# One gated add for each expert in the token mixer of a two-layer convolution and attention kernel

## The chip, the core and the metric

The kernel runs on one core of a Trainium2 chip. Its time is the device time of one execution, in microseconds (us). The numbers of the profile come from one profiled execution, and its own time stands beside them below.

## What is computed

The reference takes four images of 64 x 64 pixels with 128 channels and sends them through two layers. The first is a gated residual convolution block with a causal attention over the 4096 pixels. The second is an attention with 16 heads, a gated feed-forward part, and a mixture of 8 experts. The change is in the last of these:

```python
router_probs = jax.nn.softmax(x @ router_w + router_b, axis=-1)
top_p, top_i = jax.lax.top_k(router_probs, K)          # K = 2 of E = 8
top_p = top_p / jnp.sum(top_p, axis=-1, keepdims=True)
expert_out = jnp.einsum('bnd,edc->bnec', x, expert_w) + expert_b
gathered = jnp.take_along_axis(expert_out, top_i[..., None], axis=2)
return jnp.einsum('bnk,bnkc->bnc', top_p, gathered)
```

The kernel does not gather. It multiplies each token with all 8 experts' matrices, weights the 8 products with a row of 8 gates of which six are zero, and adds them to the token.

## The kernel before

**Work and tiles.** `fast_path` (L116) does one image at a time. An image is cut into 8 chunks of 512 tokens, so there are 32 chunks in all. Attention scores are computed for 128 keys and 512 queries and four heads at once: one step (`attention_step`, L832) has four score matmuls into two tiles `s` of 1024 columns, two exponentials on ScalarE (`e<-s`), and four value matmuls into `acc`.

**PSUM.** There are three tiles `s` of two banks each (`s_tile`, L138), one bank `acc`, and **one** bank `m` (`m_tile`, L141). All other matrix products (projections, the feed-forward part, the experts) go through this one bank while attention runs: `bank()` (L162) gives `m`, except when nothing runs beside, where it gives half of a tile `s`.

**Order.** The order of every engine is written out: the class `InOrder` (L95) makes each operation follow the one issued before it on its engine. Every operation is recorded there, so all rows of the profile carry line 105, and the reader goes by the names of the tiles. The main loop (L1224 to L1263) emits attention steps. For each it issues the scores (`do_step`, L230), then perhaps one piece of other work (`insert`, L247), and then the value products of the step two before (`finish`, L234). Which steps get a piece is decided by a budget of assumed costs when the program is built. It doesn't depend on what VectorE does with the piece.

**A chunk's last part.** `last_part` (L913) is a generator that gives such pieces. For the experts (L1021 to L1037) it takes each of the chunk's four blocks `k` of 128 tokens, and of each two halves of four experts. `halves` (L294) multiplies the 128 tokens with 512 columns of weights as two pieces of 256 columns, in two successive attention steps, and `product` (L280) cuts each into four matmuls of 32 output rows. After the second piece the bank `m` holds a 128 x 512 product, and VectorE reads it. The bank can be written again when VectorE has read it: the next piece belongs to the next half, or to the products with `eb` that end the chunk. Thirty-one of the 32 chunks run beside attention; the last of the last image runs alone at the end.

**VectorE on a product.** The 128 x 512 product is multiplied with the gates, broadcast along the channels, and written to `by_e` in SBUF. After the second half a sum over the 8 experts (a strided reduction of 128 x 1024 to 128 x 128) writes `added`, and an addition puts `added` on the tokens `t`. `by_e` shares its buffer with the tile `two` of `second_operands` (L662), and `added` with the tiles of tag `w`.

Of the kernel before, what the change touches and what calls it, by code (L numbers as in the profile page):

```python
# [9 lines left out]
FP = mybir.dt.float32  # L10
FR = mybir.dt.float32r
AF = mybir.ActivationFunctionType
ALU = mybir.AluOpType
AX = mybir.AxisListType

P = 128
C = 128
# [18 lines left out]
NE = 8  # L36
# [79 lines left out]
def fast_path(ctx: ExitStack, tc: tile.TileContext, a: dict, where: dict, out: bass.AP, verdict):  # L116
# [9 lines left out]
    pe, dve, act, pool, sp = (InOrder(tc, e) for e in (nc.tensor, nc.vector, nc.scalar, nc.gpsimd, nc.sync))  # L126
# [4 lines left out]
    wk = ctx.enter_context(tc.tile_pool(name="f_wk", bufs=2))  # L131
# [9 lines left out]
    def m_tile():  # L141
        return ps_m.tile([P, QB], FP, tag="m", name="m")
# [7 lines left out]
    def chunk(tag, name=None):  # L150
        return wk.tile([P, QB], FP, tag=tag, bufs=CHUNKS.get(tag, 1), name=name or tag)
# [4 lines left out]
    def by_k(ap):  # L156
        return ap.rearrange("p (k c) -> p k c", k=4)
# [4 lines left out]
    def bank():  # L162
        return s_tile()[:, :QB] if alone[0] else m_tile()
# [130 lines left out]
    def halves(ps, lhs, rhs, size=P):  # L294

        for h in range(2):
            cols = slice(h * QB // 2, (h + 1) * QB // 2)
            product(ps[:size, cols], lhs, rhs[:, cols])
            if h == 0:
                yield 0.46, "held"  # L300
# [531 lines left out]
    def attention_step(b, seg, kt, place, qx, vg, part):  # L832
# [19 lines left out]
        def values(es):  # L852
            for j in range(NSLOT):
                pe.matmul(
                    acc[j * SLOT : j * SLOT + 1 + HD1, :],
                    lhsT=vg[:, kt // 4, kt % 4, j, :],
                    rhs=es[j // 2][:, (j % 2) * QB : (j % 2 + 1) * QB],
                    start=kt == seg.lo,
                    stop=kt == seg.hi - 1,
                )  # L860
            if kt == seg.hi - 1:
                at = chunk("at1")
                if part:
                    dve.tensor_tensor(at, acc, part[0], ALU.add)
                else:
                    dve.tensor_copy(at, acc)
                to = scratch[b]["a"][c, g] if seg.hi == NT else scratch[b]["p"][g, c]
                sp.dma_start(out=to, in_=at)
                if seg.hi == NT and g == NG1 - 1:
                    fillers.append([last_part(b, c), LAST, (b, c), False])  # L870
# [36 lines left out]
    def fetch_following(b, c):  # L907
        keys = [part[2] for part in fillers]
        at = keys.index((b, c)) + 1
        if at < len(keys) and keys[at]:  # L910
            fetch(*keys[at])

    def last_part(b, c):  # L913
# [4 lines left out]
        ps = bank()  # L918
# [5 lines left out]
        ps = bank()  # L924
# [6 lines left out]
        for n, (lo, size) in enumerate(FCH):  # L931
            ps = bank()
# [5 lines left out]
            ps = bank()  # L938
# [4 lines left out]
        ps = bank()  # L943
        for m in range(4 * len(FCH)):
            k, n = divmod(m, len(FCH))
# [17 lines left out]
        ps = bank()  # L963
# [4 lines left out]
        ps = bank()  # L968
# [42 lines left out]
        gate = gates[:, :, :NE]  # L1011
# [8 lines left out]
            sp.dma_start(out=g8.rearrange("e (k b a) -> b e k a", k=4, a=SLOT)[b_], in_=by_block[b_, :NE])  # L1020
        for k in range(4):  # L1021
            tk = t[:, k * C : (k + 1) * C]
            by_e = wk.tile([P, NE, C], FP, tag="two", bufs=1, name="by_e")
            for half in range(2):
                ps = bank()
                yield from halves(ps, yT[:, k * P : (k + 1) * P], we_f[:, half * QB : (half + 1) * QB])
                dve.tensor_tensor(
                    by_e[:, 4 * half : 4 * half + 4, :],
                    by_k(ps),
                    gate[:, k, 4 * half : 4 * half + 4].unsqueeze(2).to_broadcast([P, 4, C]),  # L1030
                    ALU.mult,
                )
                if half == 1:
                    added = chunk("w", "added")[:, :C]
                    dve.tensor_reduce(added, by_e.rearrange("p e c -> p c e"), AX.X, ALU.add)
                    dve.tensor_tensor(tk, tk, added, ALU.add)
                fetch_following(b, c)  # L1037
                yield 0.46, "stop"
        ps = bank()
# [279 lines left out]
    ps = m_tile()  # L1319
# [5 lines left out]
    ps = m_tile()  # L1325
# [703 lines left out]
```

## Time and profile before

| | |
|---|---|
| median of three executions | 8155.83 us (8154.7 to 8157.08) |
| the profiled execution's own time | 8154.99 us |
| its span, first to last instruction | 8153.2 us |
| granted TensorE clock | 0.993 |
| busy: PE (TensorE matmul) | 7997.1 us, 98% |
| busy: ACT (ScalarE) | 7866.4 us, 96% |
| busy: DVE (VectorE) | 2415.5 us, 30% |
| busy: POOL (GpSimd) | 646.2 us, 8% |
| products `by_e<-m` beside attention | 248 of 692 ns |
| products `by_e<-s` at the end | 8 |
| sums `added<-by_e` | 128 of 1994 ns |
| additions `t<-t,added` | 128 of 293 ns |

A row of the profile names the engine, the operation, the tile written and the tiles read, the shapes (partitions x elements), how many there are, the busy time in us and the mean of one in ns. Behind the second bar stands how long the engine was idle just before these instructions, and which instruction ended most of that. PE's matmuls overlap, so a busy PE says little by itself; start times say more. In a timeline a row has its start and its length in us, and equal instructions that follow each other are merged (x8). PEld is the load of weights that goes ahead of a matmul. SPq issues the DMAs.

### The profile page before, as it was taken

The numbers are of one execution on the slowest core, as the hardware profiler recorded it, in microseconds if no ns is written. First come the engines' busy times: TensorE is split into PE (matmuls) and PEld (weight loads), VectorE is DVE, ScalarE is ACT, GpSimd is POOL, SyncE is SP. The second block draws the span as 40 slices with busy tenths as digits, with TensorE's granted clock in tenths as the row PEclk, the third lists the DMA queues.
The fourth block names the chain that finished last, engine by engine and source line by source line (L and its number), as shares of the span: only waits on it lengthen the run. The fifth ranks groups of instructions, "written<-read, shape, count | busy, mean of one in ns | idle before, by whom it ended". The sixth has DMA issues, their size and how long they took to land.

```text
span 8153.2 us, 172350 instructions
## 1 busy us (share of the span) xinstructions
PE 7997.1 (98%) x73041; PEld 2477.0 (30%) x73041; DVE 2415.5 (30%) x5001; ACT 7866.4 (96%) x8683; POOL 646.2 (8%) x592
## 2 busy tenths in 40 slices
PE   7999999999999999999999999999999999999998
PEld 3232222223333322233333332222333333232333
DVE  4333222322322232333332223333333332121123
ACT  1899999999999999999999999999999999999996
POOL 1211101000000021110000002111000000000000
PEclk9999999999999999999999999999999999999998
DMA  2221010111100000011110100101111111111121
GB/s 72 68 66 66 25 45 27 53 34 47 49 24 25 30 22 29 33 42 42 43 41 18 38 18 25 36 22 48 36 47 50 49 43 50 37 41 38 61 66 34
DMA packets 213936, 334.18 MB, mean 41 GB/s; under 512 B 31555, under 2 KB 107811, under 8 KB 213155
## 3 DMA queue, kind: packets, MB, share of 16 engines
q1 hardware_dynamic: 209139, 321.31, 12.1%
q8 instruction: 574, 9.40, 0.5%
q10 hardware_dynamic: 4016, 1.77, 0.1%
q14 instruction: 207, 1.70, 0.1%
HBM read 195.09 MB, written 127.93 MB: 40 GB/s over the span
## 4 chain that ended last, share of the span: by engine, by line
PE 90%; issue 6%; ACT 2%; DVE 1%; DMA 1%; POOL 1%; SPq 0%; ACTq 0%; POOLq 0%; DVEq 0%
PE acc L105 43%; PE s L105 29%; PE m L105 18%; ACT e L105 1%; DVE h L105 0%; DMA f_kx<-d_k 0%; POOL rs L105 0%; DVE at L105 0%; POOL xt L105 0%; ACT t L105 0%; DMA xe<-in_x_dram 0%; SPq L105 0%; ACT neg L105 0%; DVE added L105 0%; DMA taps<-in_L_conv_W_dram 0%
## 5 line engine op out<-in xcount | busy, mean ns | idle before, releaser
L105 ACT ACTIVATE e<-s 128x1024 f32<-128x1024 f32 x8480 | 7807.1, 1110 | 81.7 <-PE s L105 75.9
L105 PE MATMUL acc<-e,vg 128*9 128x512 f32 x32768 | 4334.6, 595 | 1.4 <-DVE at L105 1.4
L105 PE MATMUL s<-qx,f_kx 32*128 32x512 f32 (+1 forms) x16960 | 2890.3, 495 | 48.5 <-ACT e L105 25.9
L105 PEld LDWEIGHTS s<-qx,f_kx 32*128 32x128 f32 (+1 forms) x16960 | 1163.5, 181 | 4080.7 <-ACT e L105 3858.7
L105 PEld LDWEIGHTS acc<-e,vg 128*9 128x9 f32 x32768 | 718.4, 90 | 793.9 <-issue 456.0
L105 PE MATMUL m<-v,f_wino 128*32 128x256 f32 x5376 | 429.9, 391 | 7.3 <-POOL v L105 7.3
L105 DVE TENSOR_TENSOR by_e<-m,gates 128x512 f32<-128x512 f32 x248 | 171.5, 692 | 741.0 <-PE m L105 737.8
L105 PE MATMUL m<-f_we,y2T 128*32 128x256 f32 x3968 | 316.9, 391 | 0.5 <-DVE by_e L105 0.5
L105 POOL TENSOR_TENSOR v<-r 128x1024 f32<-128x1024 f32 x112 | 216.7, 1941 | 1264.4 <-PE m L105 1264.0
L105 DVE COPY sd<-m 128x512 f32<-128x512 f32 x168 | 116.2, 692 | 670.7 <-PE m L105 670.7
L105 POOL TENSOR_TENSOR rs<-ve,f_minus_half 128x4 f32<-128x4 f32 x64 | 65.3, 1020 | 3148.0 <-DVE ve L105 3148.0
L105 DVE COPY at<-acc 128x512 f32<-128x512 f32 x131 | 90.6, 692 | 691.5 <-PE acc L105 691.5
L105 DVE TENSOR_REDUCE added<-by_e 128x128 f32<-128x1024 f32 x128 | 255.2, 1994 | 4.8 <-DMA d_g<-turned 0.5
L105 PE MATMUL m<-hT,f_fw 128*32 128x256 f32 (+1 forms) x2728 | 236.0, 391 | 0.0
L105 POOL TENSOR_TENSOR t<-t,h 128x512 f32<-128x512 f32 x32 | 41.0, 1281 | 2036.8 <-DVE h L105 2036.8
L105 DVE TENSOR_TENSOR t<-m,sums 128x256 f32<-128x256 f32 x126 | 53.5, 425 | 493.5 <-PE m L105 493.5
L105 DVE SCALAR_TENSOR_TENSOR h<-m,h 128x512 f32<-128x512 f32 (+1 forms) x93 | 64.2, 690 | 426.9 <-ACT th L105 265.8
L105 DVE COPY h<-m 128x512 f32<-128x512 f32 (+1 forms) x93 | 64.2, 690 | 371.3 <-PE m L105 371.3
L105 DVE TENSOR_TENSOR t<-m,t 128x512 f32<-128x512 f32 x62 | 42.9, 692 | 436.7 <-PE m L105 436.7
L105 PEld LDWEIGHTS m<-v,f_wino 128*32 128x32 f32 x5376 | 105.8, 108 | 172.2 <-issue 144.3
L105 PE MATMUL m<-e,f_v 128*32 128x512 f32 (+1 forms) x1104 | 146.5, 574 | 0.0
L105 DVE TENSOR_TENSOR e<-e,f_consts 128x128 f32<-128x128 f32 x128 | 29.1, 287 | 338.8 <-ACT e L105 338.8
(250 smaller groups left out, 3308.3 us busy)
## 6 DMA issues: line engine op xcount, KB each, us to landing
f_kx<-d_k SPq DMA_DIRECT2D x139, 512.0 KB
qx<-d_q SPq DMA_DIRECT2D x152, 256.0 KB
d_q<-two SPq DMA_DIRECT2D x64, 512.0 KB
d_a<-at SPq DMA_DIRECT2D x128, 256.0 KB
vg<-d_v SPq DMA_DIRECT2D x32, 576.0 KB
d_k<-two SPq DMA_DIRECT2D x32, 512.0 KB
d_v<-vc SPq DMA_DIRECT2D x32, 288.0 KB
xe<-in_x_dram SPq DMA_DIRECT2D x32, 256.0 KB
```

What stands on the lines that cost most here:

```text
L105: made = op(*args, **kw)
```

## The change

The product and the sum are replaced: each expert's 128 x 128 part of the bank is multiplied with the token's gate for it and added to the tokens `t` in place, in one `scalar_tensor_tensor`. There are four of these for each half. `by_e` and `added` are gone. TensorE, ScalarE, GpSimd and the DMA queues have the same instructions in the same order as before. In the built program each of the last three operations of a half waits on a VectorE semaphore for the one before it, because it reads the `t` that this one wrote, and the next matmul into the bank waits for the fourth.

```diff
         for k in range(4):
             tk = t[:, k * C : (k + 1) * C]
-            by_e = wk.tile([P, NE, C], FP, tag="two", bufs=1, name="by_e")
             for half in range(2):
                 ps = bank()
                 yield from halves(ps, yT[:, k * P : (k + 1) * P], we_f[:, half * QB : (half + 1) * QB])
-                dve.tensor_tensor(
-                    by_e[:, 4 * half : 4 * half + 4, :],
-                    by_k(ps),
-                    gate[:, k, 4 * half : 4 * half + 4].unsqueeze(2).to_broadcast([P, 4, C]),
-                    ALU.mult,
-                )
-                if half == 1:
-                    added = chunk("w", "added")[:, :C]
-                    dve.tensor_reduce(added, by_e.rearrange("p e c -> p c e"), AX.X, ALU.add)
-                    dve.tensor_tensor(tk, tk, added, ALU.add)
+                for e in range(4):
+                    at = 4 * half + e
+                    dve.scalar_tensor_tensor(
+                        tk, ps[:, e * C : (e + 1) * C], gate[:, k, at : at + 1], tk, ALU.mult, ALU.add
+                    )
                 fetch_following(b, c)
                 yield 0.46, "stop"
```

## The prediction, on record before the changed kernel ran

> **What bounds the kernel now.** I read the page's busy times first, then its chain, then the timeline around the products that change.
>
> ```profile
> PE 7997.1 (98%) x73041; PEld 2477.0 (30%) x73041; DVE 2415.5 (30%) x5001; ACT 7866.4 (96%) x8683; POOL 646.2 (8%) x592
> ...
> PE 90%; issue 6%; ACT 2%; DVE 1%; DMA 1%; POOL 1%; SPq 0%; ACTq 0%; POOLq 0%; DVEq 0%
> ...
> L105 DVE TENSOR_TENSOR by_e<-m,gates 128x512 f32<-128x512 f32 x248 | 171.5, 692 | 741.0 <-PE m L105 737.8
> ...
> L105 DVE TENSOR_REDUCE added<-by_e 128x128 f32<-128x1024 f32 x128 | 255.2, 1994 | 4.8 <-DMA d_g<-turned 0.5
> ```
>
> PE and ACT share the bound: attention hands scores from one to the other. DVE is busy for 30% and on 1% of the chain, so less work on DVE is worth nothing by itself. What counts is when DVE lets go of something that PE waits for, and here that is the single bank `m`. The timeline of an ordinary expert product:
>
> ```profile
> 2142.68 0.51 PE L105 MATMUL s<-qx,f_kx 32*128 32x512 f32 x4
> ...
> 2143.12 0.64 PE L105 MATMUL m<-f_we,y2T 128*32 128x256 f32 x8
> ...
> 2143.58 1.04 PE L105 MATMUL acc<-e,vg 128*9 128x512 f32 x8
> 2143.83 0.69 DVE L105 TENSOR_TENSOR by_e<-m,gates 128x512 f32<-128x512 f32 x1 [3.04 <-PE m L105]
> ...
> 2144.55 0.51 PE L105 MATMUL s<-qx,f_kx 32*128 32x512 f32 x4
> ...
> 2144.98 0.64 PE L105 MATMUL m<-f_we,y2T 128*32 128x256 f32 x8
> ```
>
> PE's starts run 2142.68 scores, 2143.12 the piece into `m`, 2143.58 values, 2144.55 scores again: no hole, 1.87 us a step. ACT's two exponentials need less: their starts are 0.904 us apart when ACT has its input (the 25th percentile over all of them is 0.904), so 1.81 us. In steps that carry a piece PE is the bound. And the bank: DVE starts to read at 2143.83, PE writes it again at 2144.98, **1.15 us later**. Reading takes 0.69, so 0.46 us are to spare.
>
> **The change, part by part.**
>
> *What goes.* Per block of 128 tokens, two products, a sum and an addition: 2 x 0.692 + 1.994 + 0.293 = 3.67 us of DVE. *What comes.* Eight gated adds. The trace has the same operation on the same shapes, where a token is corrected from the bank (`xt<-m,rs,xt`):
>
> ```profile
> L105 DVE SCALAR_TENSOR_TENSOR xt<-m,rs,xt 128x128 f32<-128x128 f32 x116 | 35.4, 347 | 2.0
> ```
> ```profile
> 218.73 0.17 DVE L105 RECIPROCAL rs<-rs 128x2 f32<-128x2 f32 x1
> 218.94 0.61 DVE L105 SCALAR_TENSOR_TENSOR xt<-m,rs,xt 128x128 f32<-128x128 f32 x2
> ```
>
> The second row holds two that don't depend on each other: 0.61 us for both, so they overlap (0.351 and 0.343 long, the second started 0.267 after the first). The new ones are a chain through `t`, each with a wait. The nearest row of a waiting one is the first of each such pair, which waits for the reciprocal: it starts 0.035 us after that ends and takes 0.351 (58 cases). A sum and its addition show the same 0.035. So a half takes 4 x 0.351 + 3 x 0.035 = **1.509 us instead of 0.692**. Over all 128 blocks DVE is busy 8 x 0.351 = 2.81 instead of 3.67 us each, 110 us less; cover: it idles 70%, so this is worth nothing.
>
> The bank is therefore held longer, although DVE does less. After DVE's last read PE's next matmul starts 0.054 us later, wherever it really waited (26 reads of `m`, 0.053 to 0.055). From the start of reading to the earliest next write: 1.509 + 0.054 = 1.563 us. Where the next write came after 1.155 us, it is now late by **0.408 us**.
>
> *How many.* From the trace's start times I took, for each of the 248 products, the time to the next matmul into `m`: 118 have 1.0 to 1.16 us, one has 0.71, 104 have 2.8 to 3.1 and 25 more than 4.6 (there the schedule leaves a step without a piece). The last 129 have room for 1.56 us and cost nothing.
>
> *Who waits behind.* PE works in order: behind the late piece stand the values of an earlier step and the scores of the next, for which ACT waits. Whether that delay reaches the end is answered by the one product that was read late:
>
> ```profile
> 7911.85 0.50 PE L105 MATMUL s<-qx,f_kx 32*128 32x512 f32 x4
> ...
> 7912.18 0.65 DVE L105 TENSOR_TENSOR by_e<-m,gates 128x512 f32<-128x512 f32 x1
> ...
> 7912.88 0.64 PE L105 MATMUL m<-f_we,y2T 128*32 128x256 f32 x8 [0.53 <-DVE by_e L105]
> ...
> 7914.31 0.51 PE L105 MATMUL s<-qx,f_kx 32*128 32x512 f32 x4
> ...
> 7914.91 1.02 ACT L105 ACTIVATE e<-s 128x1024 f32<-128x1024 f32 x1 [0.41 <-PE s L105]
> ```
>
> PE's piece was due at 7911.85 + 0.44 = 7912.29 and came at 7912.88, 0.59 late. The next scores came 2.46 instead of 1.87 us after the last, 0.59 late, and ACT's exponentials started 1.536 instead of 0.941 us apart, 0.595 late. Nothing was absorbed. Is ACT as starved elsewhere? In 111 of the 119 places the next exponential starts within 0.61 us of the start of its score matmuls, as soon as they are done; in eight it starts 0.01 to 0.28 us later than that, which absorbs 0.9 us together. ACT, once idle, can't make it up: outside these steps it is the bound itself.
>
> So: 118 x 0.408 + (1.563 - 0.708) - 0.9 = 48.1 us more.
>
> *The end.* The last chunk runs alone, and there DVE is the chain: its first product starts at 8130.91 and the last addition ends at 8145.20, 14.29 us. The new chain of 32 adds takes 32 x 0.351 + 31 x 0.035 = 12.32: **2.0 us less**, if PE keeps up, which it does with two pieces of about 0.5 us for each half of 1.54.
>
> *What else moves.* No DMA, no matmul and no exponential changes its place. The buffers of `by_e` and `added` are free; only 0.5 us of DVE idle time was ever put down to them (the DMA of `d_g`), at the end, and it is in the 2.0. The next `m` matmul now has two waits, one in PE's sequencer ahead of it. PE's sequencer passes 540 such waits in this trace, the load behind starts 0.013 us after one (median); I take 0 and keep 0 to 0.16 us for it (0.16 is the whole weight load `m<-f_we` of the timeline). For the pitch of the chain I take 0.386 us; 0.267, the pair without a wait, is the lower end.
>
> *Sum.* 48.1 - 2.0 = +46.1 us on the profiled execution's 8154.99 (its span is 8153.2; it lies 0.8 below the median of the three runs, 8155.83): **8201 us**, 0.56% slower.
>
> *Against the skill.* The trace has 0.267 us between adds without a wait and 0.386 with one. The Trainium skill (VectorE: DVE Perf Modes, "The DRAIN you can't avoid") reports eight copies taking the same time with a semaphore after each and after the last alone, so that the wait "costs nothing extra here". By that rule a half would take 3 x 0.267 + 0.343 and the sum would be the first rival's. The row is of this very operation, so I go by it. The same page's section "The TRN2 errata" gives 120 cycles plus one for each element for a read of PSUM at 0.96 GHz; an estimate from it is 0.258 us for 128 elements, where the rows show 0.347 to 0.351. Four would be 1.03 us, inside the 1.15, and the kernel would gain about 6 us at the end.
>
> **The rivals.**
>
> 1. *The adds overlap* (not slower). If they went at 0.267 us, a half would end at 3 x 0.267 + 0.343 + 0.054 = 1.198 us, late by 0.043: 118 x 0.043 + 0.49 = 5.6 us, less what ACT absorbs, about 0.3; the end would gain 14.29 - (31 x 0.267 + 0.343) = 5.7. Net -0.4: 8154.6 us. It decides at a pitch of 0.253 us, where no product is late. For it: the pair of 0.61 us. Against: the built program has a wait at each.
> 2. *Half of the delay is absorbed*, because ACT after a late step meets a PE that gets ahead again in the next step without a piece. 24 - 2 = +22: 8177 us. Against: ACT's starved starts, and 7914.91.
> 3. *The stall costs PE more than the wait*, with the weight load no longer hidden or the double wait dear: up to 119 x 0.16 = 19 us more: 8220 us. For it: PE had its loads ahead in ordinary steps. Against: in the step of 7912.88 the values follow after 0.46 us, as always.
> 4. *DVE's relief counts* (faster): what PE's loads for `m` waited on `added` (12.7 us, 52 times) and on `at` (28.9 us, 95 times), both late behind sums of 1.99 us, goes, with the 2.0 of the end and no new wait: 8154.99 - 43.6 = 8111 us. Against: these waits are 0.24 and 0.30 us apiece, in front of a PE that is still busy with the step before.
>
> **How the numbers follow.** Forecast 0.68; rivals 0.08, 0.10, 0.12 and 0.02. Forecast and rivals 2 and 3 are slower by over 0.2% (16 us, about what a measurement of this kernel can tell from no change): 0.90. Same 0.08, faster 0.02. The range goes from just below rival 2 to rival 3, 8175 to 8220, and leaves out rivals 1 and 4 and the outer parts of 2 and 3.
>
> **What would show it.** A row of 992 gated adds `t<-m,gates,t` at 351 ns. In tight steps, adds 0.386 apart and the next `m` matmul 1.56 us after the first of them, with scores 2.27 instead of 1.87 us apart. PE's `m` waiting on DVE `t` about 119 times for 0.4 us. ACT idle on PE `s` some 25 us more than now: of the 0.595 us at 7914.91 the profile shows 0.41 as idle, so 0.408 will show as about 0.2. No change where 2.9 us lie between. I am wrong if the adds start before the one in front has ended, or if ACT's exponentials keep their 0.941 us in tight steps.

## The result, and the profile after

The changed kernel takes **8206.58 us** (median of four executions, 8205.69 to 8209.05), the kernel before beside it 8156.45 (four, 8154.7 to 8161.35). The ratio is 1.0062, with a 95% interval of 1.005 to 1.0074: 50 us, or 0.6%, slower. The forecast was 8201 us, 46 us slower.

The profiled execution after has 8205.69 us and a span of 8203.9 us, 50.7 more than before, at the same granted clock of 0.993. Its page, the busy times, the shares of the chain and the group of the new operation:

```profile
PE 8000.4 (98%) x73041; PEld 2485.2 (30%) x73041; DVE 2305.7 (28%) x5513; ACT 7877.1 (96%) x8683; POOL 646.1 (8%) x592
...
PE 88%; issue 6%; DVE 3%; ACT 2%; DMA 1%; POOL 1%; SPq 0%; ACTq 0%; DVEq 0%; POOLq 0%
...
L105 DVE SCALAR_TENSOR_TENSOR t<-m,gates,t 128x128 f32<-128x128 f32 x992 | 348.1, 351 | 847.1 <-PE m L105 817.4
```

DVE is busy for 110 us less than before, as forecast, and the kernel is 50 us slower. The busy times can't show that; only DVE's share of the chain does, which rose from 1 to 3%. The timeline of one half whose bank is written again in the next step:

```profile
2140.31 1.51 DVE L105 SCALAR_TENSOR_TENSOR t<-m,gates,t 128x128 f32<-128x128 f32 x4
...
2141.03 0.51 PE L105 MATMUL s<-qx,f_kx 32*128 32x512 f32 x4
...
2141.96 0.64 PE L105 MATMUL m<-f_we,y2T 128*32 128x256 f32 x8 [0.43 <-DVE t L105]
...
2142.39 1.07 PE L105 MATMUL acc<-e,vg 128*9 128x512 f32 x8
...
2143.39 0.51 PE L105 MATMUL s<-qx,f_kx 32*128 32x512 f32 x4
```

Four adds hold the bank for 1.51 us from 2140.31 on. PE, which wrote `m` again 1.15 us after the first read before, now does so after 1.65 us (2141.96), and everything behind it in PE's order is late: scores are 2.36 us apart (2141.03, 2143.39) instead of 1.87. From the waits of after, in us in total, times and the longest:

```profile
PE m L105 <- DVE t L105: 46.2, 105, 1.4
```

PE waits 0.44 us for the adds on average in 105 places, and hands the delay on to ACT, whose idle time on `s` rose from 75.9 us in 24 places to 120.7 in 140. The 14 other short places, where products with `eb` follow, are listed as waits of `m` on `s`: 5.4 us in 14 places, of which there are none before.

**Where the 50.7 us are.** I set the 8480 exponentials `e<-s`, which come in the same order in both traces, against each other, and took the growth of the difference between their starts.

| stretch | after minus before, us |
|---|---|
| 119 tight places (next write of `m` under 1.2 us after the read began) | +56.7 (median 0.498 each) |
| 129 loose places | +0.03 |
| the rest of the stream | -3.4 |
| before the first exponential | +0.2 |
| from the start of the last exponential on | -2.8 |

I don't put the -3.4 us down to the change. At 4944 and at 5318 to 5323 us the profiled execution of before has short stretches that are about 2.0 us longer than in the profile of `long_one` below and 4.1 us longer than in that of `long_halves`, neither of which changes anything there. In the profile of after they are about 2.5 us shorter than in that of before, which is most of the -3.4. One is a DMA wait (ACT for `xe`, 1.69 us); the cause at 5320 stays open.

### The profile page after: what moved, and what is told of

It reads as the page before. It is cut to its first block, busy times and chain, and to the rows that moved or that the text cites. A ratio compares the mean times of both kernels' runs of the same rounds, so it can differ in the third digit from the quotient of the medians.

```text
span 8203.9 us, 173097 instructions
## 1 busy us (share of the span) xinstructions
PE 8000.4 (98%) x73041; PEld 2485.2 (30%) x73041; DVE 2305.7 (28%) x5513; ACT 7877.1 (96%) x8683; POOL 646.1 (8%) x592
## 4 chain that ended last, share of the span: by engine, by line
PE 88%; issue 6%; DVE 3%; ACT 2%; DMA 1%; POOL 1%; SPq 0%; ACTq 0%; DVEq 0%; POOLq 0%
PE acc L105 41%; PE s L105 29%; PE m L105 18%; DVE t L105 2%; ACT e L105 1%; DVE h L105 0%; DMA f_kx<-d_k 0%; POOL rs L105 0%; DVE at L105 0%; POOL xt L105 0%; ACT t L105 0%; ACT neg L105 0%; SPq L105 0%; DMA xe<-in_x_dram 0%; DMA taps<-in_L_conv_W_dram 0%
## 5 line engine op out<-in xcount | busy, mean ns | idle before, releaser
L105 ACT ACTIVATE e<-s 128x1024 f32<-128x1024 f32 x8480 | 7817.9, 1108 | 125.9 <-PE s L105 120.7
L105 DVE SCALAR_TENSOR_TENSOR t<-m,gates,t 128x128 f32<-128x128 f32 x992 | 348.1, 351 | 847.1 <-PE m L105 817.4
L105 PEld LDWEIGHTS m<-f_we,y2T 128*32 128x32 f32 x3968 | 81.1, 107 | 172.1 <-issue 88.5
```

The source lines that it names most:

```text
L105: made = op(*args, **kw)
```

## The experiments

The theory: time is lost because the single bank `m` is held past the next write, and the number of VectorE operations, their waits and their sum cost nothing in themselves. The rival: the chain of waiting adds, or the wait in PE's sequencer, costs something of its own. Each diff is shortened and against the changed kernel unless it says otherwise; all kernels compute the whole result.

**1. `copy_first`: the same four adds, but out of SBUF.**

```diff
+held = wk.tile([P, 2, QB], FP, tag="two", bufs=1, name="held")[:, half, :]
+dve.tensor_copy(held, ps)
 for e in range(4):                      # reads held[...] instead of ps[...]
```

> The bank m is copied to SBUF in one operation of 128x512 (0.692 us), and the four gated adds then read the copy. VectorE has more to do than in either kernel and as many dependent adds as the changed one. If the time is lost because the bank is held (bank theory), the next matmul finds it free after 0.69 us as before the change: no late step, only the end grows, by 8 x (0.69 + 4 x 0.35 + 4 x 0.035) - 14.3 = 3.6 us: about 8160 us. If it is lost to the number of VectorE's operations or their waits, wherever the bank stands (rival): 8206 us or more.

Measured: 8160.99 us, ratio 1.0006 (0.9996 to 1.0015). The timeline of the same half:

```profile
2141.56 0.69 DVE L105 COPY held<-m 128x512 f32<-128x512 f32 x1
...
2142.28 1.51 DVE L105 SCALAR_TENSOR_TENSOR t<-held,gates,t 128x128 f32<-128x128 f32 x4
...
2142.71 0.64 PE L105 MATMUL m<-f_we,y2T 128*32 128x256 f32 x8
```

The chain of four is still there and still takes 1.51 us. But PE writes the bank 1.15 us after the copy began, while the adds run. The tight places cost 0.1 us in total and the whole stream 0.3; of the 5.0 us that the span is longer, 4.0 lie behind the last exponential, in the last chunk, where DVE is the chain and has the copies to do as well, and 0.7 ahead of the first, where the edit changes nothing. The loss is the bank's, not the chain's. The Trainium skill (VectorE: DVE Perf Modes, "Rules for kernel authors") advises to copy a product to SBUF first when many operations read it. The run agrees with the advice, though not by faster reads: an add takes 352 ns from SBUF and 351 from the bank. What the copy buys is the early release.

**2. `read_twice`: the kernel before, with its product computed twice.** The second writes the same values over the first. No gated add is in it.

```diff
+for _ in range(2):
     dve.tensor_tensor(by_e[...], by_k(ps), gate[...], ALU.mult)
```

> The kernel before, with each product by_e taken from the bank twice, the second overwriting the first; the values stay the same. There are no gated adds. Bank theory: held for 0.692 + 0.035 + 0.692 = 1.419 us; where PE's next matmul has two waits (105 tight places) it is late by 1.419 + 0.145 - 1.155 = 0.41 us, in the 14 with one by 0.32: 47 us, and some 6 us at the end, where VectorE is the chain: 8209 us. Rival, that the chain of dependent adds or 512 more operations cost the time: these are only 256 more, 8156 to 8162 us, or half the loss, about 8180.

Measured: 8203.41 us, ratio 1.0059 (1.0044 to 1.0075), and 45.4 us in the tight places (47 expected; the whole is 5.6 us under the expectation). Two reads hold the bank for 1.42 us, and the loss is back without the change. The theory and this number need no chain of adds at all.

**3 and 4. `two_chains` and `two_chains_own`: two independent chains.** The odd experts go to a tile `odd`, added to the tokens once per block, so that an add waits for the one before the last. The third kernel takes the buffer for `odd` from the tag `w`, the fourth that of the old `by_e`.

```diff
+if half == 0:
+    odd = chunk("w", "odd")[:, :C]                   # two_chains
+    odd = wk.tile([P, 2, QB], FP, tag="two", bufs=1, name="odd")[:, 0, :C]   # two_chains_own
 for e in range(4):
...
+    if e % 2 == 0:
         dve.scalar_tensor_tensor(tk, part, g, tk, ALU.mult, ALU.add)
+    elif at == 1:
+        dve.tensor_scalar(odd, part, g, None, ALU.mult)
+    else:
+        dve.scalar_tensor_tensor(odd, part, g, odd, ALU.mult, ALU.add)
+if half == 1:
+    dve.tensor_tensor(tk, tk, odd, ALU.add)
```

> The changed kernel, but the adds of odd experts go to a second tile that is added to the tokens once for each block: each add depends on the one two before it. Bank theory with the pitch of the unwaited pair (0.267 us): held for 3 x 0.267 + 0.343 = 1.144 us, late by 0.13 us in 105 places and 0.04 in 14, 15 us, and 4 us less at the end: 8167 us. If a wait costs its 0.035 us and the overlap even where its producer has ended, the pitch stays 0.386 and the time 8206 us.

Measured: 8183.89 us, ratio 1.0032 (1.002 to 1.0044), 17 us above the expectation. **A miss.** The adds did go 0.258 to 0.267 us apart instead of 0.386, and most tight places lost only 0.115 us. But where the first half of a chunk is a tight place, it lost more: in 12 of 14 such chunks 1.1 to 3.7 us, in most of them 1.4.

```profile
2145.58 0.35 DVE L105 TENSOR_SCALAR odd<-m,gates 128x128 f32<-128x128 f32 x1 [1.16 <-DMA d_g<-turned]
```

The tag `w` is also the buffer of `turned`, which a DMA is still sending to memory. DVE waits for that DMA while the bank is full: 37.5 us in 30 places by the waits of the tile `odd`. In the loose places there was room for this; PE waited for `odd` 18.7 us in 14 places. That cost belongs to my edit, so the fourth kernel takes the other buffer.

> two_chains, with the odd experts' tile in the buffer that by_e had, instead of the one from which d_g is being sent. In two_chains VectorE stood 37.5 us in 30 places waiting for that DMA with the bank held. Bank theory: what is left is the 0.115 us a place that the other places showed, 105 x 0.115 + 14 x 0.02 = 12 us, less 4 at the end: 8164 us. If the two chains themselves are what cost (rival): 8184 us again.

Measured: 8161.66 us, ratio 1.0005 (0.9996 to 1.0015). The DMA wait is gone, the tight places lose 11.4 us, and the end is 4.6 us shorter. So rival 1 of the prediction was right about its condition: at 0.26 us apart the change would have cost next to nothing. It was wrong that the adds are 0.26 apart.

**5. `by_piece`: the adds of experts 0 and 1 as soon as the first 256 columns are written.** When the bank is full, only two adds are left to do, 0.386 + 0.351 = 0.74 us.

```diff
+for h in range(2):
+    product(ps[:, cols], ...)                       # one piece of 256 columns
+    for e in range(2 * h, 2 * h + 2): add(e)
+    if h == 0: yield 0.46, "held"
```

> The changed kernel with the same 32 adds for each block, but the first two of a half are issued when the first piece of 256 columns has landed, one attention step ahead of the second. Bank theory: after the last piece only two adds hold the bank, 2 x 0.351 + 0.035 + 0.145 = 0.88 us, under 1.155: no late step, and 2 us less at the end: 8154 us, no slower than before the change. Rival (operations and their waits): 8206 us.

Measured: 8198.16 us, ratio 1.0053 (1.0039 to 1.0067). **A miss** by 44 us. The tight places are back at no loss, except at the first half of a chunk. There 28 of the 31 chunks lose 1.2 to 1.9 us, most of them 1.26, whether the place was tight or loose before:

```profile
2142.24 0.64 PE L105 MATMUL m<-f_we,y2T 128*32 128x256 f32 x8 [1.18 <-DVE t L105]
```

The adds of a chunk can't start before its `gates` are ready: DVE writes them at 2140.96, and the first two adds start at 2141.50. In the changed kernel, PE had written both pieces by then; now the second piece, in the same bank, waits for adds that wait for the gates. Another 8.8 us came behind the last exponential, where no attention lies between the pieces.

**6 and 7. `by_piece_copy` and `by_piece_alone`.** The first half of each chunk is copied whole, as in `copy_first`, and the rest goes by piece. The second of them also leaves the last chunk, which runs alone, as the changed kernel has it.

```diff
+if not first and not whole: add(ps, range(2 * h, 2 * h + 2))   # by piece
+if whole: add(ps, range(4))                                    # by_piece_alone only
+elif first: dve.tensor_copy(held, ps); add(held, range(4))
```

> by_piece, with the first half of each chunk handled otherwise, because by_piece lost its 35 us there alone: the second piece waited for adds that waited for the gates. That half is copied to SBUF in one operation (0.69 us) and added from there; all others are added by the piece. Bank theory: no late step, at the end 32 adds and one copy, 12.3 + 0.7 instead of 14.3 us: 8154 to 8156 us. If the loss in by_piece had another cause than the gates (rival): 8190 us again.

Measured: 8166.31 us, ratio 1.0013 (1.0004 to 1.0022). Half right. The stream is 0.7 us shorter than before, which settles that the loss in `by_piece` was the second piece's wait at the chunks' first halves. From the last exponential on it is 9.4 us longer, which I hadn't sized. The timeline there:

```profile
8140.37 1.59 DVE L105 SCALAR_TENSOR_TENSOR t<-s,gates,t 128x128 f32<-128x128 f32 x4 [1.32 <-PE s L105]
```

DVE waits 1.32 us for PE's piece, and that piece (at 8139.11) had waited for DVE's adds before it: the two pieces of a half share a bank, and with no other work between, a piece and its adds can't overlap.

> by_piece_copy, but the last chunk, which runs without attention beside it, is added as in the changed kernel (four adds once the whole half has landed). by_piece_copy lost 10 us there, because PE's second piece waited for the adds on the first. Bank theory: no late step beside attention and 2 us less at the end than before the change: span 8150 to 8151 us, time 8154 us. If by_piece_copy's 10 us came from its steps beside attention (rival): 8166 us again.

Measured: 8153.99 us, ratio 0.9997 (0.9988 to 1.0006): the same as before, and some 53 us less than the changed kernel. The gated add can be had at no cost, but I found no version of it that beats the kernel before.

**8. `empty_step`: the changed kernel with a step without a piece after every half.** Nothing about the adds changes; only the next write comes later.

```diff
 yield 0.46, "stop"
+yield 0.0, "stop"
```

> The changed kernel, with one empty place asked for behind each half's adds, so that a step without a piece follows and the next write into the bank comes some 2.8 us after the first add instead of 1.15. The adds and their waits are those of the changed kernel. Bank theory: no late step, 2 us less at the end, and the order of other pieces shifts: 8150 to 8162 us. Rival (operations and their waits): 8200 us or more.

Measured: 8155.3 us, ratio 0.9999 (0.9989 to 1.0008). The four adds still take 1.51 us, as after, but in the 119 places that were tight the next write now comes 2.9 us or more after the first of them (2.9 to 3.1 in 81, more in the others), and PE's matmuls into `m` never wait for `t`. The loss is gone with the adds untouched. (The pieces behind it shift to other steps, so this isn't the kernel after in everything else.)

**9 and 10. `long_one` and `long_halves`: one wait against two.** The forecast was 4.6 us low, and in 105 of the tight places PE started 0.145 us after the last read instead of 0.054. In these 105 places the changed kernel's next matmul into `m` waits on DVE and also on PE's own earlier matmuls, where before it waited on DVE alone; `read_twice` has the same. Both new kernels read the bank twice over into `held` and add from there. One does so in one operation and has one wait, the other in two and has two.

```diff
+held2 = wk.tile([P, 2, QB], FP, tag="two", bufs=1, name="held")
+dve.tensor_copy(held2, ps.unsqueeze(1).to_broadcast([P, 2, QB]))           # long_one
+for cols in (slice(0, QB // 2), slice(QB // 2, QB)):                       # long_halves
+    dve.tensor_copy(held2[:, :, cols], ps[:, cols].unsqueeze(1).to_broadcast([P, 2, QB // 2]))
```

> The bank is copied twice over into `held` (128x1024, the bank broadcast) by one operation, and the four adds read SBUF, so the next matmul into `m` has one wait, for one long read. From the copy of 512 (0.692 us) at one element in 1.04 ns the copy should take about 1.225 us, 0.07 us more than the 1.155 us to the next write. If the longer release of 0.145 us belongs to the second wait, PE's matmul starts 0.054 us after this read, 0.124 us late in 119 tight places: 15 us in the stream, about 9 us at the end, 8179 us. Rival: the release is 0.145 us wherever PE really waits long, whatever the number of waits: 0.215 us late, 26 us in the stream, 8190 us.

Measured: 8174.56 us, ratio 1.0024 (1.0014 to 1.0033), 12.4 us in the tight places and 8.3 from the last exponential on.

```profile
2141.26 1.22 DVE L105 COPY held<-m 128x1024 f32<-128x1024 f32 x1
...
2142.54 0.64 PE L105 MATMUL m<-f_we,y2T 128*32 128x256 f32 x8
```

> The same copy in two operations, one for each half of the bank's columns: the same elements are read and written, but the next matmul into `m` has two waits in the built program, on VectorE and on PE itself. Two of about 0.692 us take 1.27 us if the second starts early (it depends on nothing) and 1.42 if not. With 0.145 us from the end of the second to the matmul: 0.26 to 0.41 us late in the tight places, 31 to 48 us in the stream, 8195 to 8212 us. Rival (the number of waits doesn't matter): the release is the same as in the kernel with one copy.

Measured: 8192.0 us, ratio 1.0043 (1.0027 to 1.006), 30.3 us in the tight places: just below what was expected, 8195 to 8212, and the two copies take 1.29 us.

```profile
2143.10 1.29 DVE L105 COPY held<-m 128x512 f32<-128x512 f32 x2
...
2144.53 0.64 PE L105 MATMUL m<-f_we,y2T 128*32 128x256 f32 x8 [0.20 <-DVE held L105]
```

PE really waits in both, in the same 105 places, from the end of the last read to the first matmul 0.054 us with one wait (5 to 95%: 0.054 to 0.056) and 0.146 with two (0.146 to 0.147). The length of the wait doesn't matter; the second wait does. The median place lost 0.118 and 0.274 us: the 0.156 between them is 0.092 of release and 0.064 of a longer read.

The traces show where the time goes. With one wait, the weight load itself waits on DVE's semaphore; it starts 0.052 us after the read. With two, the load waits on PE's semaphore, and the wait on DVE stands in a semaphore event of PE's sequencer ahead of it. At 2141.817 in the profile of after the last add ends; the event runs from 2141.855 to 2141.906, the load starts at 2141.931 and the matmul at 2141.962. In the 14 tight places whose next write is `m<-f_eb`, which had two waits before and three after, the release is 0.054 in `long_one`, 0.101 in `long_halves` and 0.100 after. In `long_one` DVE's wait stands in the load there and the other one in an event ahead. So it isn't the number of waits as such that costs, but that DVE's wait, the last to end, is moved out of the load. (Why one event with two waits gives 0.100 and one with DVE's alone 0.145 stays open.)

## Why the prediction was right, and the step that failed

- **The single bank is the cost** (right). Experiments 1, 2 and 8 take the loss away with the adds kept, bring it with no adds, and take it away by the schedule.
- **1.509 us for a half** (right). 0.385 to 0.387 us between the starts of adds, 351 ns each, 1.51 us in all. In `two_chains` the adds that wait for an operation further back go 0.258 to 0.267 apart, so the wait for the operation directly in front costs 0.12 us on this operation. The Trainium skill (VectorE: DVE Perf Modes, "The DRAIN you can't avoid") has the semaphore cost nothing extra in a row of copies; for these adds the measurement says otherwise.
- **119 tight places and 129 loose ones** (right). The loose ones cost 0.03 us together.
- **0.054 us from the last read to the next matmul; the double wait "I take 0"** (wrong: this is the step that failed). It is 0.145 us in 105 places and 0.100 in 14. 105 x 0.091 + 14 x 0.046 = 10.2 us, the whole of the excess in the tight places (56.7 against 48.1 forecast) with 1.6 us to spare. Rival 3 named the mechanism and allowed up to 0.16 us for it, so the range held. That the sum came out only 4.6 us low is partly luck: the tight places were 8.6 us under, and the -3.4 us above, which I don't put down to the change, hide some of that.
  The price stood in the trace of before. I had kept only reads that PE followed within 0.08 us, and that threshold cut off 29 others that belonged beside them. The 0.013 us ran from the end of a semaphore event to the load behind it, and left out the 0.04 us from the read's end to the event, and the event itself. In the 29 places the last to read the bank are adds like those shown in the prediction (`xt<-m,rs,xt`, two from 218.94 on), which end at 219.545:

```profile
219.70 0.43 PE L105 MATMUL m<-f_w3f,at 128*32 128x129 f32 x8
```

  Three reads of one bank (a small one ahead of these two), then 0.15 us to PE's matmul (0.145 to 0.155 in all 29). Ahead of each of these matmuls PE's sequencer has a semaphore event of 51 ns. Of such events ahead of the loads `m<-f_we` there are 34 before, 27 in `long_one`, and 132 after and in `long_halves`, of which 105 wait on DVE's semaphore.
- **Nothing is absorbed but 0.9 us** (nearly right). 56.7 us is 1.6 less than 48.1 + 10.2, so by this difference some 2.5 us were absorbed.
- **The end** (right): the 32 adds take 12.17 us, forecast 12.32, instead of 14.29.
- **No relief from a less busy DVE** (right): rival 4 had 8111 us. 110 us of DVE time went, and PE's loads for `m` still wait 28.8 us in 95 places on `at`, where it was 28.9 in 95; the 12.7 us on `added` are gone and nothing moved for it.
- **The check on ACT** (wrong). I expected 25 us more idle time on `s`; it is 44.8 us (120.7 less 75.9), because I scaled from one place where 0.41 of 0.595 us showed as idle. The check on the scores, 2.27 us apart, is 2.36 for the same 0.09 us of the second wait.

## What to carry to other kernels

An edit to what empties a PSUM bank is priced by the time from the first read to the next write of that bank, and not by the busy time of the engine that reads: take the distribution of that time, add the new hold and its release, and only the places where it is short count. Read a single bank out in one operation, or leave a step free behind it; four short reads that depend on each other cost more than one long one even when their sum is less work. When a change adds a second wait to a matmul, look for a matmul in the trace that already has two, see which of them stands in the load and which ahead of it, and don't filter the slow releases out of the sample.

## What was not expected of the hardware

- A matmul that waits on DVE and on PE starts 0.145 us after DVE's last read, one that waits on DVE alone 0.054 us, whatever the length of the wait (`after`, `read_twice`, `long_one`, `long_halves`; 105 places each). In the first case DVE's wait stands in a semaphore event ahead of the load, in the second in the load itself.
- Two gated adds of 351 ns go 0.258 to 0.267 us apart when the second doesn't wait for the first, and 0.386 when it does; a wait on the operation before the last adds nothing to these 0.258 to 0.267 us (`two_chains`).
